# Layer 2's mixing: S of eight fy at a time on the whole TensorE array, in rows of four matmuls

## The chip, the cores and the metric

The kernel runs on one core of one Trainium2 chip. The metric is the device time of one execution in microseconds (us); the median of three runs before is 4785.59 us (4783.89 to 4785.9).

## The reference

Four residual layers on x (16 x 16 x 256 x 256, f32), each preceded by a group normalisation. The change is in layer 2 alone, a Laplace-operator layer in Fourier space:

```python
alpha = jnp.fft.fft2(x, axes=(-2, -1))
A  = 1.0 / (omega1[:, None, None, None] - weights_pole1[None])
Bm = 1.0 / (omega2[:, None, None, None] - weights_pole2[None])
S = jnp.einsum('ikpq,oikp,xikq->oxik', weights_residue, A, Bm)
output_residue1 = jnp.einsum('biox,oxik->bkox', alpha, S)
...
x1 = jnp.fft.ifft2(output_residue1, s=(Ny, Nx), axes=(-2, -1)).real
```

S is a complex 16 x 16 matrix for every pair of frequencies (o = fy, x = fx). "Mixing" below is the making of S and the product of alpha with it. The other residue, the transforms and the layers 0, 1 and 3 are in other stages and are the same in both kernels.

## The kernel before, in words

The stages follow one another: layers 0 and 1; layer 2's forward transform, which leaves alpha in device memory (`alphad`) and sums the residues over q into `t2`; the mixing; layer 2's way back; layer 3. The mixing takes from about 2243 to 3296 us of the span. Real input halves the work to NX = 129 columns of fx; fy comes in N = 256 rows arranged so that NF = 64 groups of four pairs of fy cover all.

TensorE, VectorE (V), ScalarE (ACT) and GpSimd (Q) run the mixing in the order in which the code is written (`manual_schedule`); only SP's queue, which issues the DMAs, is ordered by the framework. Each engine works its own list in order.

For each n (four fy):
- `poles(e8)` makes the factor A of eight fy on VectorE, in 12 steps: two differences (`ae`), a square and a sum (`ag`), a reciprocal (L852), then for each of four blocks of 32 partitions two products (`af`). It is a generator: a step is done where the main loop calls `next(coming)`. Before the change it starts at `at` = 16 of every even n, with a step at every fourth `at`.
- `masked(n, k0)` spreads A over a block pattern on GpSimd: the stationary tiles `l0` and `l1` for one half h of the input channels each (KC = 8 output channels, four operations of 256 elements per partition).
- `system(n)` makes S: for each output channel k and half h, one matmul with `l` (128 x 64) as stationary and `t2` (128 x 258) as moving operand (L887). The halves h = 0 and 1 write partitions 0 to 63 and 64 to 127 of the same PSUM tile, on two column tiles of the array. Two channels share a tile `ps_s` of two banks (two such tiles exist), which ACT copies to `sk` in one instruction (L891). It is a generator with 16 steps of two matmuls.
- The products: for each of the 129 columns x, `sk[:, x]` (128 x 32) is stationary and `z[:, :, x]` (128 x 64) is moving (L951). Four of them go to the four column tiles of the array at each of 32 places `at`; the one odd column follows at `at` = 8 (`ps_e`). Eight `at` fill a PSUM tile `ps_m` (four exist); ACT copies half of it to `other` (L964), and VectorE makes sum and difference into `ob` (helper line L190, two operations).
- `moves(n, at)`: at `at` = 1, 4, ... 22 VectorE sets one zero element of the next `z` (L940), which holds the load of that part of z on SP (L901, eight loads of 129 KB per n) until VectorE has come there. `z` has two tiles. At `at` = 2 and 5 the finished `ob` of the n before is stored (L905).

While the products of n run, `system(n + 1)` is advanced at every odd `at`: two S matmuls, then the products of two `at`. What is left of it runs at the end of n. The next n's first product needs all of its `sk` and `z`. S of n = 0 is made before the loop.

Of the kernel before, what the change touches and what calls it, by code (L numbers as in the profile page):

```python
# [46 lines left out]
F32 = mybir.dt.float32  # L51
# [114 lines left out]
def layers(ctx, tc, x, w0, w1, w3, sw, bias, ty, tx, p1a, p1b, p1c, p2a, p2b, p2c, resa, resb,  # L166
# [22 lines left out]
    def tt(eng, o, a, b, op):  # L189
        eng.tensor_tensor(o, a, b, op)  # L190
# [637 lines left out]
    with ExitStack() as es:  # L828
        ps_s = es.enter_context(tc.tile_pool(name="c_ps_s", bufs=2, space=PSUM))
        ps_m = es.enter_context(tc.tile_pool(name="c_ps_m", bufs=4, space=PSUM))  # L830

        zp = es.enter_context(tc.tile_pool(name="c_z", bufs=1))
        fp = es.enter_context(tc.tile_pool(name="c_f", bufs=2))
        lp = es.enter_context(tc.tile_pool(name="c_l", bufs=2))
        sp = es.enter_context(tc.tile_pool(name="c_s", bufs=2))
        gp = es.enter_context(tc.tile_pool(name="c_g", bufs=3))
        op = es.enter_context(tc.tile_pool(name="c_o", bufs=3))
        NF = N // 4
        FB = 4 * B // BG

        def poles(e8):

            af = afs[e8] = new(fp, [HC, 2, C, FC], "af")
            e, g = new(fp, [HC, C, FC], "ae"), new(fp, [HC, C, FC], "ag")
            for h in range(HC):
                tt(V, e[:, h], bc(wy[:, FC * e8 : FC * e8 + FC], 1, C), bc(pyi[:, h], 2, FC), SUB)
            yield
            tt(V, g, e, e, MUL)
            yield
            tt(V, g, g, bc(py2, 3, FC), ADD)  # L850
            yield
            V.reciprocal(g, g)  # L852
            yield
            for k, at in enumerate(blocks):
                tt(V, af[at, :, 1 - k % 2], e[at], g[at], MUL)
                yield
                tt(V, af[at, :, k % 2], g[at], bc(pyr, 3, FC)[at], MUL)
                yield

        KC = 8  # L860
        afs, lss, sks = {}, {}, {}

        def masked(n, k0):

            if n == NF:
                return
            ls = []
            for h in range(HC):
                l = new(lp, [KC, 4, 2, 8], f"l{h}")
                for r in range(2):  # L870
                    a = afs[n // 2][:, h, r, k0 : k0 + KC, n % 2 * 4 : n % 2 * 4 + 4]
                    tt(Q, l[:, :, :, r], bc(a, 3, 8), bc(bc(mod, 1, 4), 1, KC), MUL)
                ls.append(l.rearrange("p k f r i -> p k (f r i)"))
            lss[n, k0] = ls

        def system(n):


            sk = sks[n] = new(sp, [NX, 2 * C], "sk")
            for k0 in range(0, C, KC):  # L880
                masked(*((n, KC) if k0 == 0 else (n + 1, 0)))
                ls = lss.pop((n, k0))
                for k in range(k0, k0 + KC, 2):
                    ps = ps_s.tile([P, 2, 512], F32, tag="ps_s", name="ps_s")
                    for d in range(2):
                        for h in range(HC):
                            nc.tensor.matmul(ps[64 * h : 64 * h + 64, d, 0 : 2 * NX], lhsT=ls[h][:, k + d - k0],  # L887
                                             rhs=t2[:, h, k + d].rearrange("p x r -> p (x r)"), start=True, stop=True)
                        if d:
                            copy = V.tensor_copy if n == 0 and k % 4 else nc.scalar.copy  # L890
                            copy(sk[:, :, 2 * k : 2 * k + 4].rearrange("p x (k r) -> p x k r", r=2),  # L891
                                 ps[:, :, 0 : 2 * NX].rearrange("p k (x r) -> p x k r", r=2))
                        yield

        PX = 32
        GX = 8

        def load(n, h, f, to):

            rows_ = slice(64 * h + 16 * f, 64 * h + 16 * f + 16)  # L900
            nc.sync.dma_start(zs[n % 2][rows_, 4 * to : 4 * to + 4].rearrange("p q x b -> p (q x b)"),  # L901
                              alphad[4 * n + f, h].rearrange("r i q x b -> (r i) (q x b)"))

        def leave(n, p_):
            nc.sync.dma_start(mixd[2 * n + p_].rearrange("t k r u b g -> (t k r) (u b g)"),  # L905
                              obs[n][:, p_].rearrange("p u b g -> p (u b g)"))

        es.enter_context(tc.manual_schedule(engines={  # L910
            mybir.EngineType.PE, mybir.EngineType.DVE, mybir.EngineType.Activation, mybir.EngineType.Pool}))

        zs = [new(zp, [FB, NX, BG], f"z{k}") for k in range(2)]
        V.memset(zs[0], 0.0)
        Q.memset(zs[1], 0.0)
        for h in range(HC):
            for f in range(4):
                for to in ((0, 1) if f < 2 else (f,)):
                    load(0, h, f, to)
        for e8 in range(2):  # L920
            for _ in poles(e8):
                pass
        masked(0, 0)
        for to in range(2):
            block = zs[0][:, 4 * to : 4 * to + 4]
            V.tensor_scalar(block, block, alone[:, to : to + 1], None, MUL)
        for _ in system(0):
            pass

        def moves(n, at):  # L930

            if n and at in (2, 5):
                leave(n - 1, at // 3)
            if n == 1 and at == 0:
                Q.memset(zs[0][:, 0:8], 0.0)
            if n + 1 < NF and at % 3 == 1 and at < 24:
                part = at // 3
                h, f = part % 2, part // 2

                V.memset(zs[(n + 1) % 2][64 * h : 64 * h + 64, 4 * f, 0, 0:1], 0.0)  # L940
                load(n + 1, h, f, f)

        obs = {}
        coming = iter(())
        for n in range(NF):
            z, sk = zs[n % 2], sks.pop(n)
            steps = system(n + 1) if n + 1 < NF else iter(())

            ob = obs[n] = new(op, [2, 2, B, PX], "ob")
            def product(to, x_):  # L950
                nc.tensor.matmul(to, lhsT=sk[:, x_], rhs=z[:, :, x_], start=True, stop=True)  # L951

            for at in range(PX):
                if at % GX == 0:
                    ps = ps_m.tile([P, GX, 4 * B], F32, tag="ps_m", name="ps_m")
                if at == PX // 2 and n % 2 == 0 and n // 2 + 2 < NF // 2:
                    coming = poles(n // 2 + 2)
                moves(n, at)
                for a in range(4):
                    product(ps[32 * a : 32 * a + 32, at % GX], 1 + PX * a + at)  # L960
                if at % GX == GX - 1:
                    v = ps.rearrange("p g (n s b) -> p g n s b", n=2, s=2)
                    other = gp.tile([P, GX, 2, B], F32, tag="other", name="other")
                    nc.scalar.copy(other, v[:, :, :, 1])  # L964
                    for u, op_ in enumerate((ADD, SUB)):
                        tt(V, ob[:, :, u, :, at - GX + 1 : at + 1].rearrange("p n b g -> p g n b"), v[:, :, :, 0], other, op_)
                if at == GX:

                    first = slice(0, 32)
                    pe = ps_m.tile([P, GX, 4 * B], F32, tag="ps_m", name="ps_e")  # L970
                    product(pe[first, 0], 0)
                    alone_ = gp.tile([P, 2, 2, B], F32, tag="alone_", name="alone_")
                    V.tensor_copy(alone_[first], pe[first, 0].rearrange("p (n s b) -> p n s b", n=2, s=2))
                    for u, (op_, new_, old) in enumerate(((ADD, imag, real), (SUB, real, imag))):
                        e = gp.tile([P, 2, B], F32, tag=f"e{u}", name=f"e{u}")
                        to = ob[first, :, u, :, 0]
                        tt(Q, e[first], alone_[first, :, 0], alone_[first, :, 1], op_)
                        Q.tensor_scalar(e[first], e[first], new_[first], None, MUL)
                        Q.tensor_scalar(to, to, old[first], None, MUL)
                        tt(Q, to, to, e[first], ADD)  # L980
                if at % 2:
                    next(steps, None)
                if at % 4 == 2:
                    next(coming, None)
            for _ in steps:
                pass
        for p_ in range(2):
            leave(NF - 1, p_)

# [302 lines left out]
```

## Time and profile before

| what | value |
|---|---|
| median of three runs | 4785.59 us |
| the profiled execution, its own time | 4783.8 us |
| its span, first to last instruction | 4782.0 us |
| mean granted TensorE clock | 0.968 |
| busy over the span: PE, PEld, DVE, ACT, POOL | 92, 62, 66, 50, 44% |
| the mixing, 2243 to 3296 us: busy PE, DVE, ACT, POOL | 984, 588, 393, 494 us of 1053 |
| DMA share and rate in the mixing | 0.47, 131 GB/s |

PE is TensorE's matmuls, PEld its weight loads (which overlap them), DVE is VectorE, POOL is GpSimd, SP issues DMAs. A row of groups reads: line, engine, operation, written tile <- read tiles, shape, count | busy us, mean ns of one | idle us of the engine just before, and what ended it. A row of a timeline reads: start us, duration us, engine, line, operation, tiles, shape, count, and in brackets the idle time before it and what ended that. An f32 matmul stands in the trace as two records. The ends of matmuls are modelled, so the distance between starts is the better measure of their pace.

### The profile page before, as it was taken

How to read it: one execution, taken by the hardware profiler on the slowest of the kernel's cores; microseconds unless marked ns; L12 is line 12 of the kernel's file. 1: busy time of each engine (PE TensorE's matmuls, PEld its weight loads, DVE VectorE, ACT ScalarE, POOL GpSimd, SP SyncE). 2: the span in 40 equal slices, each digit the busy share in tenths (PEclk: the TensorE clock that was granted, in tenths of full speed). 3: DMA queues.
4: the chain of work that ended last, by engine and by line, in shares of the span. 5: the costliest groups of instructions: out<-in, count | busy, mean ns of one | idle time of the engine just before them, and what ended most of it. 6: DMA issues, size and time to landing. Idle time of an engine off the chain costs nothing. (4 is left out here: it accounts for less than half of the span.)

```text
span 4782.0 us, 121189 instructions
## 1 busy us (share of the span) xinstructions
PE 4383.6 (92%) x50448; PEld 2978.9 (62%) x50448; DVE 3136.1 (66%) x5814; ACT 2407.4 (50%) x3189; POOL 2116.4 (44%) x3297
## 2 busy tenths in 40 slices
PE   5999999999589999997999999997899999969999
PEld 2555555555369999997444444444788888844444
DVE  4676766666688787877555555553666667676664
ACT  3786776867234444443333333335444444446664
POOL 1233242332455465554444444443777777741000
PEclk9999999999799999998999999998999999989999
DMA  6686766765435444453444444446787788856664
GB/s 148 151 195 152 176 175 152 189 155 143 110 114 169 137 156 142 154 165 103 119 139 129 140 130 140 130 137 158 211 221 219 218 226 233 228 197 277 275 266 183
DMA packets 414950, 820.47 MB, mean 172 GB/s; under 512 B 41600, under 2 KB 306816, under 8 KB 382592
## 3 DMA queue, kind: packets, MB, share of 16 engines
q1 hardware_dynamic: 357056, 577.54, 43.4%
q0 software_dynamic: 57344, 235.18, 15.6%
q8 instruction: 397, 6.50, 0.6%
q14 instruction: 153, 1.25, 0.1%
HBM read 408.86 MB, written 336.07 MB: 156 GB/s over the span
## 5 line engine op out<-in xcount | busy, mean ns | idle before, releaser
L887 PE MATMUL ps_s<-t,l 128*64 128x258 f32 x4096 | 674.1, 409 | 18.8 <-POOL l L190 16.5
L413 PE MATMUL ps<-va,wt 128*64 128x512 f32 (+1 forms) x1632 | 668.8, 571 | 11.4 <-POOL va L385 9.3
L413 PE MATMUL ps<-vb,wt 128*64 128x512 f32 (+1 forms) x1632 | 666.9, 570 | 4.7 <-DMA vb<-va 4.7
L190 DVE TENSOR_TENSOR ob<-ps_m,other 128x256 f32<-128x256 f32 x512 | 281.6, 645 | 424.6 <-ACT other L964 415.8
L951 PEld LDWEIGHTS ps_m<-z,sk 128*32 128x32 f32 x16384 | 282.2, 109 | 444.1 <-issue 369.8
L891 ACT COPY sk<-ps_s 128x516 f32<-128x516 f32 x508 | 299.0, 589 | 455.3 <-PE ps_s L887 416.6
L251 PE MATMUL ps_c<-q,wt 128*128 128x512 bf16 (+1 forms) x2400 | 503.2, 371 | 17.4 <-DVE q L1190 17.4
L757 ACT ACTIVATE y<-ps_y,bc 128x384 f32<-128x384 f32 x512 | 296.9, 581 | 422.3 <-PE ps_y L755 422.2
L434 ACT ACTIVATE v<-xt,nm 32x2048 f32<-32x2048 f32 x248 | 497.1, 2004 | 9.7 <-PE ps L448 3.5
L448 PE MATMUL ps<-v,w1s 128*64 128x259 f32 x4096 | 481.6, 394 | 11.0 <-DVE v L432 6.7
L951 PE MATMUL ps_m<-z,sk 128*32 128x64 f32 x16384 | 445.3, 226 | 47.8 <-ACT sk L891 45.0
L190 POOL TENSOR_TENSOR l<-af,c_mod 128x256 f32<-128x256 f32 x512 | 319.9, 654 | 322.2 <-PE ps_s L887 314.4
L1079 PE MATMUL ps_o<-exp,fs 128*128 128x128 f32 x2048 | 403.6, 279 | 18.8 <-ACT fs L1125 18.8
L448 PEld LDWEIGHTS ps<-v,w1s 128*64 128x64 f32 x4096 | 337.0, 141 | 133.0 <-issue 24.0
L413 PEld LDWEIGHTS ps<-va,wt 128*64 128x64 f32 x1632 | 223.2, 137 | 311.3 <-issue 284.1
L251 PEld LDWEIGHTS <-wt 128*128 128x128 bf16 x2400 | 232.7, 97 | 287.6 <-issue 19.6
L1078 PE MATMUL ps_o<-c_last,zt 128*128 128x128 f32 x2048 | 402.4, 279 | 0.4
L1078 PEld LDWEIGHTS ps_o<-c_last,zt 128*128 128x128 f32 x2048 | 327.4, 196 | 62.5 <-issue 61.3
L190 POOL TENSOR_TENSOR w<-rq 128x512 f32<-128x512 f32 x256 | 320.8, 1279 | 28.3 <-ACT rq L1080 25.5
L1079 PEld LDWEIGHTS ps_o<-exp,fs 128*128 128x128 f32 x2048 | 317.7, 196 | 19.8 <-ACT fs L1125 19.8
L190 POOL TENSOR_TENSOR acc<-acc,prod 128x256 f32<-128x256 f32 x240 | 229.8, 958 | 218.0 <-DVE prod L190 208.1
L752 PE MATMUL ps_y<-c_y,qd 128*128 128x128 f32 x2048 | 314.5, 276 | 0.0
(334 smaller groups left out, 8663.5 us busy)
## 6 DMA issues: line engine op xcount, KB each, us to landing
xt<-x2d SPq DMA_DIRECT2D x256, 512.0 KB, 4.3
z<-alphad SPq DMA_DIRECT2D x516, 129.0 KB, 3.6
xt<-in_x_dram SPq DMA_DIRECT2D x256, 256.0 KB, 7.3
x2d<-x2s POOLq DMA_DIRECT2D x256, 256.0 KB, 5.0
mixd<-ob SPq DMA_DIRECT2D x128, 512.0 KB, 4.5
ot<-mixd SPq DMA_DIRECT2D x256, 256.0 KB, 7.0
x3d<-xt POOLq DMA_DIRECT2D x128, 512.0 KB, 5.7
xt<-x3d SPq DMA_DIRECT2D x64, 1024.0 KB, 8.9
```

The source lines that it names most:

```text
L190: eng.tensor_tensor(o, a, b, op)
L251: nc.tensor.matmul(o, lhsT=w, rhs=src, start=i == 0, stop=i == len(work) - 1)
L413: nc.tensor.matmul(ps[halves[h], lo:hi, :], lhsT=wt0[:, w, :], rhs=v[:, 2 * t + lo : 2 * t + hi, j : j + N], start=j == 0 and k == 0, stop ...
L434: nc.scalar.activation(to, o.xt[c][q_], AF.Identity, bias=o.g.nm[q_, 1:2])
L448: nc.tensor.matmul(ps[halves[h], k, 0:U], lhsT=o.w1[:, w : w + 64], rhs=v1[:, lo : lo + U], start=first_, stop=not first_)
L752: nc.tensor.matmul(to[:, :, a, :], lhsT=v[:, c, a, i % 2, :], start=a == 0, stop=a == 1, rhs=y1[:, a].rearrange("p (r f) -> p r f", r=2))
L757: nc.scalar.activation(y[:, c, :], ps[:, 0 : 3 * P], AF.Copy, scale=bc2[:, b, i // 2, 0:1])
L887: nc.tensor.matmul(ps[64 * h : 64 * h + 64, d, 0 : 2 * NX], lhsT=ls[h][:, k + d - k0], rhs=t2[:, h, k + d].rearrange("p x r -> p (x r)"), ...
L891: copy(sk[:, :, 2 * k : 2 * k + 4].rearrange("p x (k r) -> p x k r", r=2), ps[:, :, 0 : 2 * NX].rearrange("p k (x r) -> p x k r", r=2))
L951: nc.tensor.matmul(to, lhsT=sk[:, x_], rhs=z[:, :, x_], start=True, stop=True)
L1078: nc.tensor.matmul(ps[:, a, c, :], lhsT=zts[d][:, a, c, :], rhs=last[:, c, :], start=True, stop=False)
L1079: nc.tensor.matmul(ps[:, a, c, :], lhsT=fs[:, d, a, :], rhs=ey[:, d, c, :], start=False, stop=True)
```

## The change

- S is made for eight fy (`system(e8)`), so the stationary operand is 128 x 128 and one matmul uses the whole array; a half h of the input channels now has a PSUM tile of its own.
- One step is four matmuls in a row (two h, two channels), and a step is done at `at` = 3, 11, 19, 27: between the products of eight `at`. Eight steps over two n make the S of the next two n.
- Each PSUM tile is copied in two pieces of 64 partitions (one per n) to two `sk` tiles; with the two h that is four pieces per step. Where h and n differ, a piece goes from one half of the partitions to the other. The pool of `sk` has four tiles.
- `l` has KC = 4 output channels of eight fy instead of eight of four.
- `poles` starts at `at` = 0 of every even n and takes a step at every third `at`; `ae` and `ag` have one buffer, and `ob` two instead of three.

```diff
-        sp = es.enter_context(tc.tile_pool(name="c_s", bufs=2))
+        sp = es.enter_context(tc.tile_pool(name="c_s", bufs=4))
-        op = es.enter_context(tc.tile_pool(name="c_o", bufs=3))
+        op = es.enter_context(tc.tile_pool(name="c_o", bufs=2))
+        ep = es.enter_context(tc.tile_pool(name="c_e", bufs=1))
...
-            e, g = new(fp, [HC, C, FC], "ae"), new(fp, [HC, C, FC], "ag")
+            e, g = new(ep, [HC, C, FC], "ae"), new(ep, [HC, C, FC], "ag")
...
-        KC = 8
+        KC = 4
+        NE = N // FC
...
-                l = new(lp, [KC, 4, 2, 8], f"l{h}")
+                l = new(lp, [KC, FC, 2, 8], f"l{h}")
                 for r in range(2):
-                    a = afs[n // 2][:, h, r, k0 : k0 + KC, n % 2 * 4 : n % 2 * 4 + 4]
-                    tt(Q, l[:, :, :, r], bc(a, 3, 8), bc(bc(mod, 1, 4), 1, KC), MUL)
+                    a = afs[e8][:, h, r, k0 : k0 + KC]
+                    tt(Q, l[:, :, :, r], bc(a, 3, 8), bc(bc(mod, 1, FC), 1, KC), MUL)
...
-            sk = sks[n] = new(sp, [NX, 2 * C], "sk")
+            for n in range(2):
+                sks[2 * e8 + n] = new(sp, [NX, 2 * C], "sk")
             for k0 in range(0, C, KC):
-                masked(*((n, KC) if k0 == 0 else (n + 1, 0)))
-                ls = lss.pop((n, k0))
+                masked(*((e8, k0 + KC) if k0 + KC < C else (e8 + 1, 0)))
+                ls = lss.pop((e8, k0))
                 for k in range(k0, k0 + KC, 2):
-                    ps = ps_s.tile([P, 2, 512], F32, tag="ps_s", name="ps_s")
-                    for d in range(2):
-                        for h in range(HC):
-                            nc.tensor.matmul(ps[64 * h : 64 * h + 64, d, 0 : 2 * NX], lhsT=ls[h][:, k + d - k0],
+                    for h in range(HC):
+                        ps = ps_s.tile([P, 2, 512], F32, tag="ps_s", name="ps_s")
+                        for d in range(2):
+                            nc.tensor.matmul(ps[:, d, 0 : 2 * NX], lhsT=ls[h][:, k + d - k0],
                                              rhs=t2[:, h, k + d].rearrange("p x r -> p (x r)"), start=True, stop=True)
-                        if d:
-                            copy = V.tensor_copy if n == 0 and k % 4 else nc.scalar.copy
-                            copy(sk[:, :, 2 * k : 2 * k + 4].rearrange("p x (k r) -> p x k r", r=2),
-                                 ps[:, :, 0 : 2 * NX].rearrange("p k (x r) -> p x k r", r=2))
-                        yield
+                            if d:
+                                for n in range(2):
+                                    copy = V.tensor_copy if e8 == 0 and n else nc.scalar.copy
+                                    copy(sks[2 * e8 + n][64 * h : 64 * h + 64, :, 2 * k : 2 * k + 4]
+                                         .rearrange("p x (k r) -> p x k r", r=2),
+                                         ps[64 * n : 64 * n + 64, :, 0 : 2 * NX].rearrange("p k (x r) -> p x k r", r=2))
+                    yield
...
-            steps = system(n + 1) if n + 1 < NF else iter(())
+            if n % 2 == 0:
+                steps = system(n // 2 + 1) if n + 2 < NF else iter(())
...
-                if at == PX // 2 and n % 2 == 0 and n // 2 + 2 < NF // 2:
+                if at == 0 and n % 2 == 0 and n // 2 + 2 < NE:
                     coming = poles(n // 2 + 2)
...
-                if at % 2:
+                if at % 8 == 3:
                     next(steps, None)
-                if at % 4 == 2:
+                if at % 3 == 2:
                     next(coming, None)
-            for _ in steps:
-                pass
+            if n % 2:
+                for _ in steps:
+                    pass
```

More of the change, by code (lines that the diff above doesn't have):

```diff
@@ L858, in poles, with masked @@
                 yield
-        KC = 8
+        KC = 4
+        NE = N // FC
         afs, lss, sks = {}, {}, {}
-        def masked(n, k0):
-            if n == NF:
+        def masked(e8, k0):
+            if e8 == NE:
                 return
@@ L868, in masked @@
             for h in range(HC):
-                l = new(lp, [KC, 4, 2, 8], f"l{h}")
+                l = new(lp, [KC, FC, 2, 8], f"l{h}")
                 for r in range(2):
-                    a = afs[n // 2][:, h, r, k0 : k0 + KC, n % 2 * 4 : n % 2 * 4 + 4]
-                    tt(Q, l[:, :, :, r], bc(a, 3, 8), bc(bc(mod, 1, 4), 1, KC), MUL)
+                    a = afs[e8][:, h, r, k0 : k0 + KC]
+                    tt(Q, l[:, :, :, r], bc(a, 3, 8), bc(bc(mod, 1, FC), 1, KC), MUL)
                 ls.append(l.rearrange("p k f r i -> p k (f r i)"))
-            lss[n, k0] = ls
@@ L876, in system @@
-        def system(n):
-            sk = sks[n] = new(sp, [NX, 2 * C], "sk")
+            lss[e8, k0] = ls
+        def system(e8):
+            for n in range(2):
+                sks[2 * e8 + n] = new(sp, [NX, 2 * C], "sk")
             for k0 in range(0, C, KC):
-                masked(*((n, KC) if k0 == 0 else (n + 1, 0)))
-                ls = lss.pop((n, k0))
+                masked(*((e8, k0 + KC) if k0 + KC < C else (e8 + 1, 0)))
+                ls = lss.pop((e8, k0))
                 for k in range(k0, k0 + KC, 2):
-                    ps = ps_s.tile([P, 2, 512], F32, tag="ps_s", name="ps_s")
-                    for d in range(2):
-                        for h in range(HC):
-                            nc.tensor.matmul(ps[64 * h : 64 * h + 64, d, 0 : 2 * NX], lhsT=ls[h][:, k + d - k0],
+                    for h in range(HC):
+                        ps = ps_s.tile([P, 2, 512], F32, tag="ps_s", name="ps_s")
+                        for d in range(2):
+                            nc.tensor.matmul(ps[:, d, 0 : 2 * NX], lhsT=ls[h][:, k + d - k0],
```

## The prediction

> **What bounds the kernel now.** I read the page first (groups by line), then the timeline of TensorE in layer 2's mixing (about 2277 to 3294 us of a 4782.0 us span), then busy time by stretch, then VectorE, GpSimd and SP in the same stretch. Line numbers are those of the kernel before. From the page:
>
> ```profile
> L887 PE MATMUL ps_s<-t,l 128*64 128x258 f32 x4096 | 674.1, 409 | 18.8 <-POOL l L190 16.5
> L951 PE MATMUL ps_m<-z,sk 128*32 128x64 f32 x16384 | 445.3, 226 | 47.8 <-ACT sk L891 45.0
> L891 ACT COPY sk<-ps_s 128x516 f32<-128x516 f32 x508 | 299.0, 589 | 455.3 <-PE ps_s L887 416.6
> ```
>
> Each f32 matmul is two records (2048 S matmuls, 4096 records). TensorE never waits long here; the order of its work is the bound. TensorE over one n (four fy), and the next n's start:
>
> ```profile
> 2606.40 0.66 PE L887 MATMUL ps_s<-t,l 128*64 128x258 f32 x4
> 2606.99 0.43 PE L951 MATMUL ps_m<-z,sk 128*32 128x64 f32 x16
> 2607.35 0.66 PE L887 MATMUL ps_s<-t,l 128*64 128x258 f32 x4
> ...
> 2612.08 0.66 PE L887 MATMUL ps_s<-t,l 128*64 128x258 f32 x4
> 2613.45 0.43 PE L951 MATMUL ps_m<-z,sk 128*32 128x64 f32 x16 [0.71 <-ACT sk L891]
> ```
>
> A step is 0.945 us: 0.585 from S to products, 0.36 back. Sixteen steps, one odd product round and 0.78 us at the end, where the next n's products wait for the last S copy, make 16.02 us. The stretches show one n each (us, then busy us of PE, PEld, DVE, ACT, POOL, clock, DMA share, GB/s):
>
> ```profile
> 2597.43:2613.45 16.02, 15.31 (x322) 7.56 (x322) 8.34 (x23) 6.20 (x12) 7.32 (x17) 1.00 0.49 135
> 2613.45:2629.48 16.03, 15.31 (x323) 7.57 (x323) 9.76 (x26) 6.20 (x12) 7.81 (x17) 1.00 0.45 134
> ```
>
> How much of a step is streaming? Full-array f32 matmuls of layer 2's way back give the rate:
>
> ```profile
> 3339.33 1.12 PE L1123 MATMUL ps_f<-exp,gall 128*128 128x512 f32 x2
> 3340.29 0.38 PE L1078 MATMUL ps_o<-c_last,zt 128*128 128x128 f32 x2
> 3340.51 0.39 PE L1079 MATMUL ps_o<-exp,fs 128*128 128x128 f32 x2
> ```
>
> Two records of 128 columns start 0.22 us apart from the next two: 0.112 each. L1123's two records start 0.533 apart, and the next L1078 starts 0.429 after the second: 512 columns stream in 0.427 (0.83 ns a column), and the first after a change of tile shape costs 0.106 more. So 258 columns stream in 0.215 and a full S matmul in 0.430; a row of 8 product records (two groups of four column tiles) in 0.213. Of a step, 0.585 - 0.430 = 0.155 and 0.36 - 0.213 = 0.147 are the two changes of shape. That is 32 changes, 4.8 us of every 16.02.
>
> [...]L1078 and L1079 keep 0.112 us a record though a 128x128 f32 load lasts 0.192. [...]see af below (1.79 us against 0.42 alone). Its consequence is the largest term of my forecast.
>
> **The change, TensorE.** S of eight fy takes the whole array: 1024 matmuls instead of 2048, but the two halves ran side by side before, so streaming stays equal (16 x 0.430 us per n). What goes is the changes of shape: 8 per n, not 32. One group of 8 fx becomes:
> - four S matmuls (8 records) in a row: first record 0.215 + 0.106, six at 0.218 (0.215 plus the 0.003 that L1123 shows above streaming), last record to the first product 0.315 as now: 1.94 us;
> - 16 rounds of four products at 0.056, with the 0.08 start and 0.167 end that a step shows now: 0.08 + 14 x 0.056 + 0.167 = 1.03 us.
>
> Together 2.97, against 4 x 0.945 = 3.78. One n is 4 x 2.97 + 0.06 = 11.95 us if nothing waits.
>
> **ACT.** 1024 copies of 64 partitions replace 512 of 128; per partition the work is the same 516 elements, and I take the same 0.589 us each. For less than that nothing speaks; the upper bound is in rival 3. Their pace in a row is not shown for L891; zt copies (L1069, 0.585 us) start as close as 0.477, so I take 0.48. A group: the first pair is ready 1.19 us after S starts (last record 0.755 + 0.435 as now), copies start at 1.19, 1.67, 2.15, 2.63, then "other" (0.372) at 3.11. Sum 4 x 0.48 + 0.26 = 2.2 of 2.97: ACT has room, but the ob operations of VectorE now start 3.5 us after S does (other + 0.40). The wait for sk at a boundary comes once in two n and would be 0.35 us; it hides under the next point.
>
> **GpSimd.** The l operations stay 512 of 0.65 us. Each set is asked for two steps (5.9 us) before use and takes 2.6: no wait. The pool c_o with two buffers waits for a store issued an n earlier (landing 4.6 us): nothing. The same VectorE writes e and g, so c_e with one buffer costs nothing.
>
> **What is late next: the z loads.** VectorE's memset (L940) releases each z load on SP, and the last three (at = 16, 19, 22) stand behind ob of at 15 in VectorE's queue, with steps of poles between them. Now:
>
> ```profile
> 2621.12 1.11 DVE L190 TENSOR_TENSOR ob<-ps_m,other 128x256 f32<-128x256 f32 x2 [1.56 <-ACT other L964]
> 2622.28 0.06 DVE L940 MEMSET z<- 64x1 f32 x1
> 2622.37 1.79 DVE L190 TENSOR_TENSOR af<-ae,ag 32x256 f32<-32x256 f32 x1
> 2624.22 0.06 DVE L940 MEMSET z<- 64x1 f32 x1
> 2624.32 0.41 DVE L190 TENSOR_TENSOR af<-ag,pyr 32x256 f32<-32x256 f32 x1
> 2624.34 0.06 DVE L940 MEMSET z<- 64x1 f32 x1
> ```
> ```profile
> 2621.52 2.37 POOL L190 TENSOR_TENSOR l<-af,c_mod 128x256 f32<-128x256 f32 x4
> ```
> ```profile
> 2624.70 0.40 SPq L901 DMA_DIRECT2D z<-alphad  x1
> ...
> DMA to landing us min/median/max: 2.8/3.5/5.7
> ```
>
> The load of 2624.70 lands at about 2628.2; TensorE would begin the next n at 2628.70 and is held for sk until 2629.48. So the cover is half a microsecond, and the change takes four from the n.
> - Odd n (poles almost done): S of at 11 starts at T. ob of 15 at T + 3.5; its pair and the memsets end at T + 4.9; the three loads are issued 0.4 apart, the last at T + 5.5; + 3.5 landing + 0.1 = T + 9.1. TensorE is there at T + 2 x 2.97 + 1.94 + 0.47 = T + 8.35. It waits 0.7.
> - Even n: poles now starts at at 0 and does 10 of its 12 steps there: ae 0.93, ag 0.60 and 0.42, reciprocal 1.75, af pairs of 0.85 + 0.46, in all 7.6 us; with four ob pairs of 1.15 and small ones VectorE has 13.2 us of work in an n of 11.95. Counted from S of at 3: ob of 7 ends at 4.7, alone and ag 5.3, memset and reciprocal 7.2, af 7.8 to 8.2, ob of 15 to 9.2, memset, af (against GpSimd's l, 8 to 10.4), memset, af, and the memset of at 22 at about 11.2. Issue, 3.5 landing, 0.1: 14.8; TensorE is there at 11.4. It waits 3.4. With af never hindered 2.1, with two of them at 1.79 about 4.8.
>
> A pair of n: 2 x 11.95 + 0.7 + 3.4 = 28.0 us, against 32.05.
>
> **Ends.** Before the first n, S is now made for eight fy: eight steps of two products' halves, with half the copies on VectorE, which (as now) comes free only near 2270; I count 2 us a step from there with one more for the slow start, so the first n begins near 2286.5, not 2277: +9.5. n = 62 now has no S and takes 8.4 (its own z chain), not 16.02; the last n keeps 7.1.
>
> **Sum.** From the first n's start: before 63 x 16.02 + 7.1 = 1016.4. After 31 x 28.0 + 8.4 + 7.1 = 883.5, + 9.5 = 893. Gain 123 us. The profiled execution took 4783.8 (span 4782.0), 1.8 under the median of 4785.59: 4661 in its terms, 4662 in the median's; I say **4660**. In general the gain is 991 - 31 x pair. Nothing outside this stage is touched. A measurement tells from no change about 0.2%, 10 us.
>
> **Rivals.**
> 1. The z loads are not late (VectorE gets through, or landing falls to 2.8): pair 24.2 (with the sk wait), gain 241, 4543. For it: ACT, GpSimd and DMA (2.1 MB per n, 175 GB/s, while 202 GB/s stands in a later stage) have room. Against: the half microsecond of cover. With the stalls halved, 26: 4600. Chance 0.2.
> 2. They are later than I think: af at 1.79 twice in each even n and landing 4.5, as some loads take when stores are in flight, or weight loads that don't hide at all in the row (0.106 more per record, +6 us per pair, partly in the shadow of the loads): pair 30.4, gain 49, 4735. Chance 0.18.
> 3. Slower: a copy from one half of the partitions to the other could cost more than 0.589 us. No such copy is in the trace. ACT then paces the group: 4 copies + 0.37. From 0.86 us a copy on, a group is over 3.8 and the gain is gone; at 1.0, a group is 4.37, a pair 35.0, the time 94 over: 4878. [...]I give it 0.05.
> 4. The change doesn't do what it says: the change of shape costs as much per row of four as four changes did. L1078 and L1079 in long rows speak against it. Pair about 32: 4784. Chance 0.02.
>
> My forecast has 0.55 (pairs of 27 to 29.2, 4629 to 4697). The range 4590 to 4730 leaves out the lower half of rival 1, the end of rival 2, and 3 and 4, about 0.2. Faster 0.93, same 0.02, slower 0.05.
>
> **What would show it.** Right: S records at 0.218 in rows of eight; a group of 2.97 us between waits; L951 waiting for z loads, 3 us and below 1 in turn; ACT sk 1024 copies at 0.59; ob later after its products than now. Wrong: n of 12 us with no wait for z (rival 1); S rows well over 1.94 us (weights); copies over 0.6 us, with PE waiting for sk or ps_s (rival 3).

## The result and the profile after

After the change the kernel takes 4848.12 us (median of four runs, 4847.22 to 4852.14) against 4784.74 before: ratio 1.0134, interval 1.0117 to 1.0152. It is 63 us slower (1.3%), where 123 us of gain were forecast. The profiled execution took 4848.74 us, its span 4847.0, at a mean granted clock of 0.947.

The groups that answer to L887, L951 and L891 (line, engine, operation, tiles, count | busy us, mean ns of one | idle us before, what ended most of it), from the page of the kernel after:

```profile
L894 ACT COPY sk<-ps_s 64x516 f32<-64x516 f32 x1008 | 587.5, 583 | 411.2 <-PE ps_s L889 376.4
...
L889 PE MATMUL ps_s<-t,l 128*128 128x258 f32 x2048 | 571.7, 426 | 25.6 <-POOL l L189 16.9
...
L956 PE MATMUL ps_m<-z,sk 128*32 128x64 f32 x16384 | 317.1, 228 | 231.6 <-DVE z L944 149.8
```

TensorE works less than before: S keeps it busy for 572 us instead of 674, the products for 317 instead of 445. But the idle time before the products is 232 us instead of 48, and most of it (150 us) is no longer put down to ACT's `sk` but to VectorE's memset of `z` (L944). One pair of n in the stretches (us, then busy us of PE, PEld, DVE, ACT, POOL, clock, DMA share, GB/s) is 34.06 us where the forecast had 28.0 and the kernel before 32.05:

```profile
2701.78:2719.47 17.69, 12.19 (x290) 9.67 (x291) 14.10 (x32) 10.82 (x20) 7.18 (x16) 0.95 0.38 121
2719.47:2735.84 16.37, 14.56 (x290) 11.25 (x291) 4.81 (x17) 10.81 (x20) 7.17 (x16) 0.84 0.49 133
```

The granted clock fell too: 1.00 before, 0.95 and 0.84 here. TensorE's timeline over the end of the even n and the odd n (start us, us, operation, count, and in brackets the idle time and what ended it) shows both losses:

```profile
2707.37 1.10 PE L956 MATMUL ps_m<-z,sk 128*32 128x64 f32 x64
2708.40 2.01 PE L889 MATMUL ps_s<-t,l 128*128 128x258 f32 x8
2710.34 1.10 PE L956 MATMUL ps_m<-z,sk 128*32 128x64 f32 x64
2711.37 2.01 PE L889 MATMUL ps_s<-t,l 128*128 128x258 f32 x8
2713.31 0.65 PE L956 MATMUL ps_m<-z,sk 128*32 128x64 f32 x32
2719.47 1.08 PE L956 MATMUL ps_m<-z,sk 128*32 128x64 f32 x32 [5.51 <-DVE z L944]
2720.49 3.81 PE L889 MATMUL ps_s<-t,l 128*128 128x258 f32 x8
2724.22 0.91 PE L956 MATMUL ps_m<-z,sk 128*32 128x64 f32 x40
...
2733.39 0.65 PE L956 MATMUL ps_m<-z,sk 128*32 128x64 f32 x32
2735.84 0.37 PE L956 MATMUL ps_m<-z,sk 128*32 128x64 f32 x12 [1.80 <-DMA z<-alphad]
```

Between waits a group of eight fx is what was forecast: row 1.94 us (2708.40 to 2710.34), products 1.03 (2710.34 to 2711.37), together 2.97. At the starts of the n stand waits of 5.51 and 1.80 us. After the long one the first half round of products takes 1.02 us (start to start) where 0.58 is usual, and the row of S 3.73 instead of 1.94, at the same eight records. In just this stretch, from the end of the long wait to the end of the slow row, the granted clock (the number before the last two) is 0.50:

```profile
2719.47:2724.20 4.73, 4.73 (x40) 3.36 (x40) 0.93 (x4) 1.17 (x2) 0.00 (x0) 0.50 0.70 237
```

What ends the long wait is the last load of `z`, though the profile names a memset. At 17 of the 18 odd starts between 2370 and 2960 us TensorE goes on 0.24 or 0.30 us after that load lands, while its distance from the end of the memset named, already one for the next n, varies from 0.04 to 0.39. The load that lands is in turn held by an earlier memset.

Where did the 5.51 us begin? VectorE's timeline in the same even n, whose first row of S starts at 2702.37:

```profile
2706.41 1.14 DVE L189 TENSOR_TENSOR ob<-ps_m,other 128x256 f32<-128x256 f32 x2 [2.97 <-issue]
2707.35 0.25 DVE L978 COPY alone__24087<-ps_e 32x64 f32<-32x64 f32 x1
...
2710.31 1.08 DVE L189 TENSOR_TENSOR ob<-ps_m,other 128x256 f32<-128x256 f32 x2
2711.45 0.06 DVE L944 MEMSET z<- 64x1 f32 x1
2711.53 3.97 DVE L189 TENSOR_TENSOR af<-ag,pyr 32x256 f32<-32x256 f32 x1
2715.45 0.06 DVE L944 MEMSET z<- 64x1 f32 x1
2715.56 0.41 DVE L189 TENSOR_TENSOR af<-ae,ag 32x256 f32<-32x256 f32 x1
2716.03 0.06 DVE L944 MEMSET z<- 64x1 f32 x1
```

One `af`, an operation that takes 0.42 us alone, lasts 3.97 and stands ahead of the last two memsets; the load that the memset of 2716.03 releases is issued at 2716.12 and lands at 2719.23, and TensorE goes on at 2719.47. GpSimd in that time, with the eight small operations on the odd column (`alone`) that it does first:

```profile
2707.68 0.31 POOL L189 TENSOR_TENSOR e<-alone__24087 32x32 f32<-32x32 f32 x1 [6.65 <-DVE alone__24087 L978]
...
2710.52 4.71 POOL L189 TENSOR_TENSOR l<-af,c_mod 128x256 f32<-128x256 f32 x8
```

Two sets of `l` (x8) run in a row for 4.71 us, not one (x4) for 2.4 as before. The run ends at 2715.23 and the `af` about 0.28 us later, as in the prediction's lines of the kernel before (2624.16 against 2623.89). And the `ob` at 2706.41, with `alone` behind it, waited for ACT; it begins 0.09 us after `other` ends, so the smaller pool of `ob` is not what holds it:

```profile
2703.54 2.38 ACT L894 COPY sk<-ps_s 64x516 f32<-64x516 f32 x4 [2.14 <-PE ps_s L889]
2705.95 0.37 ACT L969 COPY other<-ps_m 128x256 f32<-128x256 f32 x1
```

**Theory A**, made from this: one chain sets the time of the load. Four copies on ACT -> `other` -> `ob` -> `alone` (VectorE) -> eight small operations (GpSimd) -> the first `l` set, late by so much that the second set is free by then and follows at once -> `af` of VectorE shut out for both -> memset of `z` -> load -> TensorE, whose clock then falls as well (0.50 above). **Rival B**: the doubled copies of 64 partitions themselves cost the time. Other rivals put it on the full-width matmuls, on the steps of `poles` or on the DMA traffic. Where the expectations below name further letters, they say what each holds.

### The profile page after: what moved, and what is told of

It reads as the page before. It is cut to its first block, busy times and chain, and to the rows that moved or that the text cites. A ratio compares the mean times of both kernels' runs of the same rounds, so it can differ in the third digit from the quotient of the medians.

```text
span 4847.0 us, 118033 instructions
## 1 busy us (share of the span) xinstructions
PE 4257.1 (88%) x48400; PEld 3160.5 (65%) x48400; DVE 3165.8 (65%) x5826; ACT 2696.4 (56%) x3689; POOL 2094.4 (43%) x3297
## 5 line engine op out<-in xcount | busy, mean ns | idle before, releaser
L894 ACT COPY sk<-ps_s 64x516 f32<-64x516 f32 x1008 | 587.5, 583 | 411.2 <-PE ps_s L889 376.4
L889 PE MATMUL ps_s<-t,l 128*128 128x258 f32 x2048 | 571.7, 426 | 25.6 <-POOL l L189 16.9
L189 DVE TENSOR_TENSOR ob<-ps_m,other 128x256 f32<-128x256 f32 x512 | 270.3, 607 | 453.8 <-issue 253.8
L956 PE MATMUL ps_m<-z,sk 128*32 128x64 f32 x16384 | 317.1, 228 | 231.6 <-DVE z L944 149.8
L956 PEld LDWEIGHTS ps_m<-z,sk 128*32 128x32 f32 x16384 | 265.8, 114 | 332.7 <-DVE z L944 165.2
L889 PEld LDWEIGHTS ps_s<-t,l 128*128 128x128 f32 x2048 | 402.5, 207 | 110.6 <-POOL l L189 19.4
L189 POOL TENSOR_TENSOR l<-af,c_mod 128x256 f32<-128x256 f32 x512 | 304.0, 622 | 33.3 <-PE ps_s L889 22.6
```

The costliest lines, as they stand in the source:

```text
L889: nc.tensor.matmul(ps[:, d, 0 : 2 * NX], lhsT=ls[h][:, k + d - k0], rhs=t2[:, h, k + d].rearrange("p x r -> p (x r)"), start=True, stop=True)
L894: copy(sks[2 * e8 + n][64 * h : 64 * h + 64, :, 2 * k : 2 * k + 4] .rearrange("p x (k r) -> p x k r", r=2), ps[64 * n : 64 * n + 64, :, 0 ...
```

## The experiments

Twelve kernels, most of them with one edit. The last three columns are us per n, from the first to the last n that starts between 2300 and 3050 us of each trace: "per n" is the mean distance of the starts of n; "waits" is the idle time of TensorE right before products, at the start of an n or within it; "slow rows" is what the rows of S take above their usual time, idle time within them included. In before and b_free 0.71 us of the waits is the one for `sk` at the start of each n that the prediction shows. One run stands where no interval is given; the kernel before took 4784 to 4785.5 us beside all of them.

| kernel | us | ratio to before | per n | waits | slow rows |
|---|---|---|---|---|---|
| before | 4784.7 | | 16.02 | 0.71 | 0.07 |
| after | 4848.1 | 1.0134 [1.0117, 1.0152] | 17.02 | 3.72 | 0.91 |
| a_early | 4727.2 | 0.9881 [0.9865, 0.9898] | 15.04 | 1.89 | 0.67 |
| a_l_once | 4747.0 | one run | 15.22 | 2.27 | 0.68 |
| a_one_copy | 4686.8 | one run | 14.42 | 1.83 | 0.33 |
| b_rows | 4753.9 | 0.9937 [0.9923, 0.9952] | 15.79 | 2.71 | 0.89 |
| a_free | 4647.7 | 0.9706 [0.9690, 0.9722] | 13.77 | 0.97 | 0.23 |
| b_rows_free | 4671.9 | 0.9763 [0.9747, 0.9778] | 14.08 | 1.11 | 0.65 |
| b_free | 4814.9 | 1.0065 [1.0050, 1.0080] | 16.52 | 1.02 | 0.16 |
| a_fill | 4801.4 | one run | 16.12 | 0.97 | 0.26 |
| a_at7 | 4624.5 | one run | 13.35 | 1.26 | 0.09 |
| a_poles4 | 4846.3 | one run | 17.04 | 3.74 | 0.90 |
| a_early_st | 4674.5 | one run | 13.98 | 1.25 | 0.28 |
| b_rows_act | 4571.3 | 0.9552 [0.9536, 0.9568] | 12.68 | 0.34 | 0.23 |

**a_early: the memsets and loads early.** From the kernel after:

```diff
-            if n + 1 < NF and at % 3 == 1 and at < 24:
-                part = at // 3
+            if n + 1 < NF and at < 8:
+                part = at
```

> The changed kernel, with the eight z loads of the next n released at at = 0 to 7, ahead of VectorE's first ob, instead of at = 1, 4, ... 22. Theory A (TensorE's new idle time is the wait for z loads, which stand late in VectorE's queue; all else of the change works as forecast): the waits of 5.5 and 1.75 us per pair of n vanish, and with them the slower clock after the long one; a pair falls from 34.0 to about 24.3 us, the time to 4540 to 4580 us. Theory B (the doubled ACT copies hold PSUM and other): little moves, above 4800 us. Theory C (the loads land late because loads and stores fill the DMA queues): the loads still arrive last, above 4750 us.

Measured: 121 us faster than after, but not the 4540 to 4580 of Theory A. At the end of even n there is no wait any more: the loads are released ahead of the slow `af`'s end. But odd n end with waits of 1.8 to 6.3 us, 3.1 in the median (TensorE's timeline there):

```profile
2734.91 0.65 PE L956 MATMUL ps_m<-z,sk 128*32 128x64 f32 x32
2738.78 1.08 PE L956 MATMUL ps_m<-z,sk 128*32 128x64 f32 x32 [3.22 <-DVE z L944]
2739.79 3.81 PE L889 MATMUL ps_s<-t,l 128*128 128x258 f32 x8
```

VectorE comes to these memsets only 3.6 us after the n starts, behind the `ob` of the n before. Eight loads and two stores then leave SP together; from the first issue (2727.13) to the last landing (2738.58) it takes 11.5 us, and the last six loads land 5.0 to 5.6 us after issue. So the late release in even n costs time, which this run shows; but Theory A was wrong to expect nothing behind it.

**a_l_once: GpSimd without the `l` work.**

```diff
-            if e8 == NE:
+            if e8 or k0 > KC:
                 return
...
-                ls = lss.pop((e8, k0))
+                ls = lss[0, k0 % (2 * KC)]
```

> The changed kernel with GpSimd's l made for the first eight fy and two sets of output channels only and used again for all others: the other l operations are left out, so S is wrong after the first. Theory A[...]: the even n's wait falls from 5.5 to about 2 us, the clock stays up, the pair is near 28.5 us, the time about 4675 us. Theory B (ACT copies) and C (DMA): no change beyond 15 us, about 4845.

Measured: 101 us faster than after; no `af` is held any more. The two behind the `ob` of 15 (VectorE's timeline in this kernel):

```profile
2648.84 0.42 DVE L189 TENSOR_TENSOR af<-ae,ag 32x256 f32<-32x256 f32 x1
2649.32 0.06 DVE L944 MEMSET z<- 64x1 f32 x1
2649.41 0.42 DVE L189 TENSOR_TENSOR af<-ag,pyr 32x256 f32<-32x256 f32 x1
2649.88 0.06 DVE L944 MEMSET z<- 64x1 f32 x1
```

So the shutting out of `af`, with what follows from it, is worth about 101 us. It isn't the whole loss: waits of 1.8 and 2.6 us (medians of even and odd starts) and slow rows remain, and A's 4675 is missed by 72 us.

**a_one_copy: one copy of 128 partitions per PSUM tile.**

```diff
-                                for n in range(2):
-                                    copy = V.tensor_copy if e8 == 0 and n else nc.scalar.copy
...
+                                copy = V.tensor_copy if e8 == 0 and h else nc.scalar.copy
+                                copy(sks[2 * e8 + h][:, :, 2 * k : 2 * k + 4].rearrange("p x (k r) -> p x k r", r=2),
+                                     ps[:, :, 0 : 2 * NX].rearrange("p k (x r) -> p x k r", r=2))
```

> The changed kernel with one ACT copy of 128 partitions per PSUM tile instead of two of 64: the halves are not sorted to their n, so S is mixed up, but matmuls, tiles and waits stay and ACT has half of the copies. Theory A: other and ob come about 1.2 us earlier after S, so the odd n's wait falls from 1.75 to about 0.6; the even n's wait is held by GpSimd and stays over 4; a pair about 32.5, the time about 4800 us. Theory B (the doubled copies are the cause): a pair of 25 to 28, 4560 to 4660 us. Theory C: about 4840.

Measured: 161 us faster than after, outside both forecasts: 113 below A's 4800 and 27 above the end of B's range (4660), so nearer to B. But in the kernel after the copies' own time is not on TensorE's path: the last of the even n's copies ends at 2714.9, and ACT is idle from 2715.3 on, while TensorE waits until 2719.47. What the copies do is to set when the chain begins. With two copies ahead of `other` instead of four, `alone` comes earlier, and the two sets of `l` part (GpSimd's timeline in this kernel):

```profile
2708.65 2.37 POOL L189 TENSOR_TENSOR l<-af,c_mod 128x256 f32<-128x256 f32 x4
2711.78 2.38 POOL L189 TENSOR_TENSOR l<-af,c_mod 128x256 f32<-128x256 f32 x4 [0.75 <-PE ps_s L889]
```

In the gap VectorE gets its `af` through, in 1.7 us, at times 2.0. So A had the chain, and had undervalued its head. What decides between A and B is a_at7 below: it keeps all the copies of 64 partitions and is faster still.

**b_rows: the kernel before, with rows of four steps and nothing else.**

```diff
-                if at % 2:
-                    next(steps, None)
+                if at % 8 == 3:
+                    for _ in range(4):
+                        next(steps, None)
```

> The kernel before with its own S (64-column matmuls, copies of 128 partitions) but four of its steps done together at at = 3, 11, 19, 27: a row of eight half-width matmuls between the products of eight at, nothing else changed. Theory A: the changes of tile shape are the whole gain of TensorE, so an n is again 12 us if nothing waits; z loads are late here too, but poles stands where it stood and ACT has half the copies, so waits of 1 to 2.5 us per n remain: a pair of 26 to 29, 4595 to 4690 us. If the width of the array were what saves TensorE time: no gain, about 4784 us.

Measured: 31 us faster than before, not the 95 to 190 expected. TensorE's row of the same S on half the columns each, and its wait:

```profile
2711.37 1.97 PE L887 MATMUL ps_s<-t,l 128*64 128x258 f32 x16
2713.27 1.10 PE L951 MATMUL ps_m<-z,sk 128*32 128x64 f32 x64
2714.30 1.97 PE L887 MATMUL ps_s<-t,l 128*64 128x258 f32 x16
...
2719.65 0.65 PE L951 MATMUL ps_m<-z,sk 128*32 128x64 f32 x32 [2.80 <-DVE z L940]
```

The row takes 1.90 us, the group 2.93. The saving of the tiling changes needs the rows alone: the whole array, the copies of 64 partitions and the four `sk` bring nothing to it. And without any of them the load of `z` is late as well, at the start of every n (waits of 2.0 to 3.6 us). Here too an `af` ahead of the memsets is held, by one set of `l` that begins with it (VectorE, then GpSimd):

```profile
2712.75 2.62 DVE L190 TENSOR_TENSOR af<-ae,ag 32x256 f32<-32x256 f32 x1
2712.72 2.37 POOL L190 TENSOR_TENSOR l<-af,c_mod 128x256 f32<-128x256 f32 x4
```

**a_free, b_rows_free and b_free: the loads not tied to VectorE.** In the kernel after, in b_rows and in the kernel before:

```diff
-            if n and at in (2, 5):
-                leave(n - 1, at // 3)
+            if n and at in (8, 11):
+                leave(n - 1, at // 9)
...
-            if n + 1 < NF and at % 3 == 1 and at < 24:
-                part = at // 3
+            if n + 1 < NF and at < 8:
+                part = at
...
-                V.memset(zs[(n + 1) % 2][64 * h : 64 * h + 64, 4 * f, 0, 0:1], 0.0)
```

> The changed kernel without the memsets of VectorE that hold the z loads: the eight loads of the next n are released at at = 0 to 7 by TensorE alone, and the two stores of ob come behind them in SP's queue (at = 8 and 11 instead of 2 and 5). Theory A (z loads late through VectorE's queue, then through the stores in front of them, are what the forecast got wrong): no wait for z above 0.5 us, no slow rows, a pair of n of 24.3 to 25.5 us, 4545 to 4590 us. Theory D (VectorE itself, 18 us busy plus its waits for GpSimd in a pair, is the bound behind it): waits for ps_m take their place, a pair of 26 to 27.5, 4600 to 4650 us. Theory C (DMA volume is the bound): waits for z remain, over 4680 us.

> The kernel before with four steps of its S in a row at at = 3, 11, 19, 27 and with the z loads released by TensorE alone at at = 0 to 7, the stores behind them. Theory A: an n of about 12 us (4 x 2.92 + 0.06, and 0.3 for sk), a pair of 24, 4530 to 4560 us; faster than the changed kernel with the same loads, since ACT has half the copies. Theory D: a pair of 26, about 4595 us. Theory C: over 4680 us.

> A control: the kernel before with the z loads released by TensorE alone at at = 0 to 7 and the stores behind them, its S steps as they were. All theories: TensorE's order is the bound here and no z load is late, so the time stays at 4784 us within 8.

Measured: a_free is 200 us faster than after; no start of an n waits for `z` any more. That the time was lost in the release of the loads is shown. But A's 4545 to 4590 is missed. The time lies in D's range (4600 to 4650), though not for D's reason: what appears is not waits for `ps_m` but waits without a releaser in the profile, within the products (timeline of TensorE in a_free):

```profile
2658.49 0.97 PE L955 MATMUL ps_m<-z,sk 128*32 128x64 f32 x50
2659.93 0.42 PE L955 MATMUL ps_m<-z,sk 128*32 128x64 f32 x14 [0.47 <-issue]
```

b_rows_free has them too and missed its forecast by over 110 us; b_free, expected equal, is 30 us slower than before. So in b_free the loads that leave in one burst at the start of an n, with the stores behind them, have a price of their own (4814.9 us against 4784.4), which the kernel before with its spread loads doesn't pay. Between 2300 and 3050 us a_free has 42 waits of TensorE above 0.4 us without a releaser, and all 42 end 0.6 to 1.9 us after a packet of the queue that the page lists as `q8 instruction` ends, times that make up 22% of the stretch; the kernel before has no such wait. Whether the one causes the other, no run tests.

**a_fill: the clock.** Twelve more matmuls of 128 x 128 at the end of even n, whose result nobody reads:

```diff
+            if n % 2 == 0 and n + 2 < NF:
+                ps = ps_s.tile([P, 2, 512], F32, tag="ps_s", name="ps_fill")
+                for i in range(12):
+                    nc.tensor.matmul(ps[:, i % 2, 0 : 2 * NX], lhsT=t2[:, 0, 0, 0:64].rearrange("p x r -> p (x r)"),
+                                     rhs=t2[:, 0, 1].rearrange("p x r -> p (x r)"), start=True, stop=True)
```

> The changed kernel with twelve more 128x128 f32 matmuls at the end of every even n, where TensorE waits for z; their result is not read. If the slow S row after the long wait (3.8 us instead of 2.0) comes from TensorE having been idle: added work takes it away and the pair falls by about 2 us, from 34.05 to 32, the time to about 4785 us. If the slow row has another cause (the loads or VectorE): no change, or some us more, 4845 to 4870 us.

TensorE's timeline in this kernel:

```profile
2656.93 5.49 PE L993 MATMUL ps_fill<-t 128*128 128x258 f32 x24
2662.83 0.65 PE L956 MATMUL ps_m<-z,sk 128*32 128x64 f32 x32 [0.41 <-DVE z L944]
2663.41 2.01 PE L889 MATMUL ps_s<-t,l 128*128 128x258 f32 x8
```

Measured: with 5.49 us of added work per pair it is 47 us faster than after, 16 us short of the 4785 forecast. The wait is filled (at most 0.4 us is left of it), and the S row behind it takes its usual time. That the slow row comes from TensorE's idleness is shown; 47 / 31 = 1.5 us per pair is what it is worth at least. Some slow rows remain behind the waits at the other end of the pair.

**a_at7 and a_poles4: where the rows and the steps of `poles` stand.**

```diff
-                if at % 8 == 3:
+                if at % 8 == 7:
                     next(steps, None)
```

```diff
-                if at % 3 == 2:
+                if at % 4 == 2:
                     next(coming, None)
```

> The changed kernel with its S rows at at = 7, 15, 23, 31 instead of 3, 11, 19, 27, so that ACT's copy other stands ahead of the four S copies in ACT's queue and not behind them. Theory A (four copies at 0.59 us push other, ob, alone and GpSimd's l back until two sets of l run together and hold VectorE): ob comes 0.85 us earlier, the sets of l part, the even n's wait falls from 5.6 to about 3.5 and the odd one's from 1.85 to 1; the next pair's sk costs up to 1 us: a pair of 29 to 31 us, 4700 to 4755 us. Rival (the order on ACT plays no part): 4840 to 4870 us.

> The changed kernel with a step of poles at every fourth at instead of every third: 8 of its 12 steps in the even n, not 10, and one instead of two between ob of at 15 and the last memset. Theory A (one af that stands behind ob and runs into GpSimd's l waits for the whole run, however many steps there are): the even n's wait falls by about 0.6 us only, a pair of 33.3, about 4825 us. Rival (the sum of poles' work in the even n is what makes the memsets late): 2.5 to 3 us less, a pair of 30.5 to 31.5, 4735 to 4770 us.

Measured: a_at7, one digit, is 224 us faster than after and 3.3% faster than before, 76 us below the lower end of A's range (4700): the direction was forecast, but at most two thirds of the size. Now `ob` of 15 comes after one row of S of its n, not two, and `other` is not behind that row's copies. It starts 6.4 us after the n does, not 8.5, the memset of `at` = 22 comes at 9.8, not 14.25, and between the two `l` sets GpSimd is idle for 2.26 us:

```profile
2643.69 2.38 POOL L189 TENSOR_TENSOR l<-af,c_mod 128x256 f32<-128x256 f32 x4
2648.32 2.74 POOL L189 TENSOR_TENSOR l<-af,c_mod 128x256 f32<-128x256 f32 x4 [2.26 <-PE ps_s L889]
```

The waits that remain are 1.0 us for `sk` at even starts (the last row now stands at the end of the n) and 0.6 to 2.0, mostly for `z`, at odd ones, and one row alone is slow. a_poles4 changed nothing (2 us), nearer to A's 4825 than to its rival's 4735 to 4770: in the even n the two `l` sets still run together, and now another `af` is held for the whole run (VectorE, then GpSimd):

```profile
2672.07 4.37 DVE L189 TENSOR_TENSOR af<-ae,ag 32x256 f32<-32x256 f32 x1
2671.46 4.71 POOL L189 TENSOR_TENSOR l<-af,c_mod 128x256 f32<-128x256 f32 x8
```

How many steps VectorE does in the even n is not the point, but when GpSimd's run. The other half of this edit, that `poles` starts at `at` = 0 and not at 16, was not taken back in any run on the kernel after.

**a_early_st: a_early with the stores later.**

```diff
-            if n and at in (2, 5):
-                leave(n - 1, at // 3)
+            if n and at in (8, 11):
+                leave(n - 1, at // 9)
```

> The run a_early (memsets and loads at at = 0 to 7) with the two stores of ob behind the loads, at at = 8 and 11 instead of 2 and 5. If what held the loads there was the stores in front of them in SP's queue and in the DMA engines: near a_free, a pair of 27.5 to 28.5, 4640 to 4675 us. If it was that VectorE comes to the memsets late at the start of an odd n: no change, about 4727 us.

Measured: at the upper end of the first forecast, 53 us faster than a_early. The two stores ahead of the loads on SP's queue were a part of what a_early lacked.

**b_rows_act: rows alone, and ACT holds the loads, spread over the n.** From b_rows:

```diff
-            if n and at in (2, 5):
-                leave(n - 1, at // 3)
+            if n and at in (17, 20):
+                leave(n - 1, (at - 17) // 3)
...
-            if n + 1 < NF and at % 3 == 1 and at < 24:
-                part = at // 3
+            if n + 1 < NF and at % 2 == 0 and at < 16:
+                part = at // 2
...
-                V.memset(zs[(n + 1) % 2][64 * h : 64 * h + 64, 4 * f, 0, 0:1], 0.0)
+                nc.scalar.mul(zs[(n + 1) % 2][64 * h : 64 * h + 64, 4 * f, 0, 0:1], imag[64 * h : 64 * h + 64], 0.0)
```

> The kernel before with rows of four S steps, z loads held by ACT (a write of zero in place of VectorE's memset) at at = 0, 2, ... 14, and the stores at at = 17 and 20: the loads are spread over half an n by an engine that is 45% busy. If the short waits in b_rows_free and a_free for which the profile names no releaser come from loads and stores in one burst[...]: they go, an n is 12.1 to 12.7 us, 4555 to 4600 us. If not: they stay, over 4640 us.

Measured: as forecast, 4.5% faster than before and the fastest of all. Most of the waits within the products are gone: between 2300 and 3050 us 12 above 0.4 us remain, 8.8 us in sum, where b_rows_free has 42 of 49.2 us. The run changes three things at once against b_rows_free (who releases the loads, how they are spread, and where the stores stand), so it doesn't say which of them does it. The stretch of 750 us (columns as above) has a clock of 1.00 and TensorE busy for 720 us:

```profile
2300.00:3050.00 750.00, 719.98 (x19002) 484.54 (x18998) 560.64 (x910) 460.55 (x1181) 447.05 (x946) 1.00 0.72 169
```

## Why the prediction was wrong, step by step

Right were the bound, the sizes of the change on TensorE (1.94, 1.03, 2.97), the cost of a copy of 64 partitions (583 ns; 589 were taken, so rival 3 is false though its sign came true), TensorE's arrival at the odd boundary (T + 8.36 against T + 8.35), and that the `z` loads are late next. Wrong is the pair, by 6.06 us in the one shown (34.06 against 28.0) and by 5.75 in the mean of all 31 (33.75):

- **The even n's step "af (against GpSimd's l, 8 to 10.4)" failed: +2.1 us.** Up to there the list held: the `ob` of 15 ran from 7.9 to 9.0 us after S of `at` = 3 (forecast to 9.2), and GpSimd's set began at 8.15. But a second set followed at once, so the run lasted to 12.9, not 10.4, the `af` behind the `ob` to 13.1 (2715.50), and the memset of `at` = 22 came at 13.7, not 11.2. The wait was 5.5, not 3.4. The upper end taken (two `af` of 1.79, 4.8 us) was too low as well. The prediction asked whether GpSimd has time, and not where in time its second set lies: in a_one_copy that set begins 10.2 us after S of `at` = 3 (2711.78, S at 2701.55), so the list's own end of the first, 10.4, would have met it. The trace shows the VectorE operation waiting for the whole run of queued GpSimd operations, 3.97 us behind eight. The prediction's own line has it already: its `af` of 1.79 lasts until a run of four is over. That the `af` is held by the `l` operations is shown by a_l_once; that the second set makes it long is seen in a_at7 and a_one_copy, where the sets part and this `af` takes 1.7 us, in a_one_copy sometimes 2.0.
- **ACT's pace was mis-sized:** 0.48 us was taken from other copies; these start 0.60 apart (2703.54, 2704.14, 2704.75, 2705.34) and take 0.583, so they don't overlap in a row, and why is open. So `other` comes 3.58 us after S, not 3.11, and `ob` at 4.04, not 3.5. It moves the odd boundary and, by way of `alone`, the first `l` set. a_one_copy and a_at7 show how much hangs on when that chain begins.
- **Odd n: +1.1 us.** The step was right in kind: `ob` of 15 at T + 3.98 (ACT's pace again), and the last load landed 4.1 us after its issue, not 3.5. The wait was 1.80, not 0.7.
- **A term was missing: the clock, +2.2 us.** After 5.5 us of idleness the row of S took 3.73 us (+1.79) and the products before it 1.02 instead of 0.58 (+0.44), at a granted clock of 0.50. The prediction put no such price on its own forecast wait of 3.4. Between 2310 and 3250 us the kernel after has 28 waits of 3.5 to 5.9 us, and a slow row follows each; after its 28 waits of 1.6 to 2.15 none does. Shown by a_fill.
- About 0.6 us of the pair is left. By the lines shown some 0.36 of it is only where a wait is counted from (an estimate: the trace's modelled end of the last products lies 0.18 us behind the 0.47 after which the forecast lets the next begin, twice in a pair); 0.14 is products still slow after the slow row (0.91 us for 40 records instead of 0.77).
- **The ends were mis-sized too, by some 12 us in all.** The first n began at 2295.37, not 2286.5: the steps of S before it took some 2.6 us each, not 2, with waits for the copies between them, and the second came only at 2275.36. n = 62 took 12.4 us, not 8.4. So it is chance that the prediction's formula with the pair of 34.05 that the first runs showed, 991 - 31 x 34.05 = -65, comes out at the measured -63: the pairs' mean and the ends differ from it in opposite directions.

Of the rivals, 2 had part of the mechanism (`af` held and loads later than thought) with too low an end (4735), and slower was given 0.05 for a reason that didn't occur. The cover that was lost, half a microsecond, was seen; that lateness feeds on itself (the clock, the sets running together) was not.

What stays open: what the waits without a releaser in the kernels with bursts of loads are; why ACT's copies to `sk` don't overlap (0.60 us apart at 0.583); and what the earlier start of `poles` costs by itself. A whole-array kernel with loads held by ACT and spread as in b_rows_act wasn't tried.

## What to carry to other kernels

When a stage is shortened by a quarter, redo the queues of all engines on the new time axis, operation by operation, GpSimd's too: what one engine loses behind another's run (here 3.97 us for an `af` of 0.42) hangs on where the two meet, not on their sums. Ask what a forecast wait of TensorE costs behind it as well: in the kernel after a slow row followed each of the 28 waits of 3.5 us and more (2.2 us lost on the 5.5 shown), and in the other kernels some of the shorter ones, down to 1.70. And tie a load's release to an engine whose list has nothing late ahead of it, spread out: rows alone were worth 31 us, rows with such a release 213.

## What was not expected of the hardware

- A VectorE operation shut out by GpSimd's `l` came through only behind the whole run: in the traces of before, after, b_rows, a_at7, a_one_copy and a_poles4 all 169 `af` of over 1 us between 2310 and 3250 us end 0.28 us after the last `l` of a run. Within a run these follow without a gap (each lasts 0.615 us and the next starts after 0.585).
- Copies from PSUM on ACT in a row start 0.60 us apart at 0.583 each, while the zt copies of 0.585 in the kernel before, also from PSUM, started as close as 0.465.
- A copy from one half of the partitions to the other costs what a straight one does: 0.580 to 0.586 us for both in the kernel after, and 0.589 for 128 partitions in the kernel before.
- S on two column tiles of 64 in rows (1.90 us) is as fast as on the whole array (1.94).
- A slow row of S can follow a shorter wait than in the kernel after. In a_early a row took 3.42 us after a wait of 2.00. In a_l_once a row is slow after a wait of 1.70 us (granted clock 0.56), and another after one of 2.78 is not (1.00); in b_rows a wait of 2.97, in a_early_st one of 3.42 had no slow row behind it.
- Loads of 129 KB landed 3.3 us after issue in the median of the kernel after, where they are spread, and 5.1 to 5.5 in the four kernels with eight of them at the start of an n (a_early, a_free, b_rows_free, b_free).
